# A graph kernel's edge sort: operand layouts, a 32-bit rank copy, a bias by product, and new ticks for the picks

## The chip, the cores and the metric

The kernel runs on one core of a Trainium2 chip. A core has five engines that work through queues of their own: PE (TensorE, matrix products; the loading of its stationary operand is listed as PEld), DVE (VectorE, element-wise work and reductions), ACT (ScalarE, activations and copies), POOL (GpSimd, here indirect transfers) and SP (SyncE, which starts transfers). Products land in PSUM, a memory of eight banks of 512 fp32 values for each of 128 partitions; everything else lies in SBUF. The metric is the device time of one execution in microseconds (us).

## What is computed

Two graph layers over 12,500 nodes of 256 features and 200,000 edges, each with a residual and a layer norm. The change concerns the first layer:

```python
feat = relu(einsum('nd,ohdk->ohnk', feat_in, W) + b[:, :, None, :])
feat_self, feat_nei = feat[0], feat[1]
att_s = leaky(einsum('hnk,hk->hn', feat_self, a_self))
att_n = leaky(einsum('hnk,hk->hn', feat_nei, a_neigh))
edge_w = (att_s[:, row] + att_n[:, col]) * adj_vals
msgs = edge_w[..., None] * feat_nei[:, col, :]
agg = segment_sum(msgs, row, num_segments=N)
...
x = layernorm(x + L0(x, src, dst, edge_weight, ...))
x = layernorm(x + L1(x, edge_index, ...))
```

Here `row` is `src`, `col` is `dst`, and the edges come sorted by `dst`. The sum of the first layer goes over `src`, so the edges have to be brought into another order.

## The kernel before, in words

The kernel has three stages. The first computes the features of the first layer and writes one message per edge into a table in memory (`log`), ordered by the block of 128 source nodes to which the edge belongs. The second reads that table block by block, sums the messages and finishes the first layer. The third is the second layer. All lines of the change lie in the first stage.

The first stage works on groups of 14 tiles of 128 edges; there are 112 groups (`NG`). For each group, `feat_tasks` computes the features of a window of 128 nodes: `transposes` (PE), `keep` (ACT copies them out of PSUM), `project` (PE, L428), `bias` (DVE, L436, adds the bias row), `relu` (ACT, L439), then the attention sums, the centring and, for the first 98 groups, the normalised part of the node block.

`sort_tasks` sorts the group's edges by source block:

- `widen` (ACT, L530) copies each edge's block number 99 times, `hot` (DVE, L534) compares it with 0..98 and so gives the one-hot matrix `A`; `halves` (DVE) adds up its tiles.
- `ranks`, `quarter`, `rows`, `begins` (PE, ACT, DVE, PE) count the edges of each block, round up to rows of four, and give each block's first row and, in the PSUM region `V`, each partition's first place in each block.
- `vhigh` (ACT) and `vlow` (DVE, L571) split `V` into two bf16 parts, which `place_mm` (PE, L588 and L590) spreads over the group's tiles and to which it adds 4096 at each edge's own block. `place_max` then picks that entry: for tiles 0 to 9 by an activation with an accumulator each (ACT, L621), for tiles 10 to 13 by a maximum (DVE, L617, L618). The result is the edge's place among 128 x 16.
- `shift`, `reach`, `steps`, `steps_keep`, `target`, `index` give the row numbers of the table to which the group's rows go.
- `split` (DVE) splits the place into a partition `q` and a column `r`; `hot_r`, `goods`, `hot_q` (DVE, L634, L639, L644) make one-hot matrices of both and multiply the column's by the five values of an edge (`em`); `permute` (PE, L650) is 14 products that put the values in their places.
- `rel_keep`, `extras` (ACT, and DVE L666, L667) read the result. The edge's position in the node window goes through memory (`rel_turn`, `rel_row`, `rel_out`, `rel_in`) and comes back on all partitions; `hot_n` (DVE, L678) makes the one-hot `oT` of it.
- `message(0..5)` (PE, L686) takes the rows of the node features with `oT`, `evict(0..5)` (ACT, L693) copies them into `m`, and `scatter(0..3)` (POOL, L699) writes `m` to the table.

The order on every engine is written by hand. A task has a tick relative to its group; a group begins each 8 ticks (`TG`). Tasks of one tick are issued by group, oldest first, and within a group as listed, sort before features. So about four groups are in work at once, and each engine goes strictly through its own queue. Tasks of the edge data (`meta_tasks`, once per nine groups: load, transpose, block number, the five values, and `twins`, which finds edges of the same block and partition) are issued last in their ticks.

PSUM tiles come by name in turns: `fs` (features, counts and the permuted values of a group), `tp` (transposes), `wp` (places) and `mp` (messages) have two banks each. A new tile waits until all readers of the one that had its bank are done. `ranks` is what takes a group's `fs` bank.

Of the kernel before, what the change touches and what calls it, by code (L numbers as in the profile page):

```python
# [26 lines left out]
P = 128  # L27
# [54 lines left out]
def kernel(  # L82
# [38 lines left out]
    NBX = NB + 1  # L121
    GR = P * NR // RW
# [73 lines left out]
    with ExitStack() as l0:  # L196
# [12 lines left out]
        iotar = dcp.tile([P, NR, GT], BF, name="iotar")  # L209
        later = dcp.tile([P, GT, GT], BF, name="later")  # L210
        identb = dcp.tile([P, P], BF, name="identb")
        identk = dcp.tile([P, P], BF, name="identk")
# [21 lines left out]
        nc.vector.tensor_copy(identb, ident)  # L234
        nc.vector.tensor_single_scalar(identk, ident, BIG, op=OP.mult)
# [5 lines left out]
        nc.vector.tensor_single_scalar(iotar, iotac[:, 0:NR, None].to_broadcast([P, NR, GT]), 0.5 - NR / 2, op=OP.add)  # L241
# [48 lines left out]
        def meta_tasks(c):  # L290
# [4 lines left out]
            def pad():  # L295
                blk[c] = meta.tile([P, TC], BF, name="blk")
                em[c] = meta.tile([P, 5, TC], BF, name="em")
# [4 lines left out]
            def column(i):  # L302
                def f():
# [4 lines left out]
                    st["pt"] = ps.tile([P, 512], FT, name="tp")  # L308
# [14 lines left out]
            def place():  # L323
                nc.vector.scalar_tensor_tensor(em[c][:, 1, :nt], st["s"][:, :nt], -float(P), srcf[:, t0:t0 + nt],
                                               op0=OP.mult, op1=OP.add)
                if full < nt:
                    nc.vector.memset(blk[c][E % P:, full:nt], -1.0)

            def high():
                nc.scalar.copy(em[c][:, 2, :nt], st["adj"][:, :nt])  # L330

            def rest():
                nc.vector.tensor_tensor(st["adj"][:, :nt], st["adj"][:, :nt], em[c][:, 2, :nt], op=OP.subtract)

            def mid():
                nc.scalar.copy(em[c][:, 3, :nt], st["adj"][:, :nt])

            def low():
                nc.vector.tensor_tensor(em[c][:, 4, :nt], st["adj"][:, :nt], em[c][:, 3, :nt], op=OP.subtract)

            def windows():
# [10 lines left out]
                nc.vector.tensor_single_scalar(em[c][:, 0, :nt], rel[:, t0:t0 + nt], 1.0, op=OP.add)  # L352
                if full < nt:
                    nc.vector.memset(em[c][E % P:, 0, full:nt], 0.0)
# [36 lines left out]
        def feat_tasks(g):  # L391
# [12 lines left out]
            def transposes():  # L404
                tp = ps.tile([P, 512], FT, name="tp")
# [18 lines left out]
            def project():  # L424
                fp = bank[g][:, 0:D] if ww else ps.tile([P, 512], FT, name="fs")[:, 0:D]
                for o in range(o0, o1):
                    for c in range(2):
# [3 lines left out]
                            start=(c == 0), stop=(c == 1))  # L431
                st["fp"] = fp

            def bias():
                st["R"] = feat.tile([P, D], FT, name="R")
                nc.vector.tensor_tensor(flat(st["R"]), st["fp"][:, lo:hi], b0b[:, lo:hi], op=OP.add)  # L436

            def relu():
# [1108 lines left out]
```

## Time and profile before

| what | value |
|---|---|
| median of 3 runs | 4602.55 us (4601.2 to 4603.93) |
| the profiled execution | 4600.86 us, its span 4599.1 us |
| PE busy | 3994.0 us, 87% of the span |
| DVE busy | 3407.1 us, 74% |
| ACT busy | 2396.9 us, 52% |
| POOL busy | 2478.5 us, 54% |
| first stage | from the start to about 1,640 us |

The span is the time from the first to the last instruction in the profile. A busy share is a mean over the three stages. In the first stage (400 to 1600 us) PE was busy 1078.8 of 1200 us, DVE 925.7, ACT 759.9 and POOL 374.6, and the mean granted clock of PE was 0.89 of full speed. In lists of instruction groups a row gives line, engine, operation, output and inputs, shapes and count, then busy us and mean ns of one, then the engine's idle time just before them and what ended it. Operations that follow each other on an engine overlap by some hundredths to a tenth of a microsecond. Ends of products are modelled, and an fp32 product is listed as two pieces.

### The profile page before, as it was taken

To read this page: it belongs to the slowest core of one execution; us is meant where nothing else is said; L and a number is where in the kernel's file an instruction comes from. 1 tells how busy PE (TensorE), PEld (TensorE's weight loads), DVE (VectorE), ACT (ScalarE), POOL (GpSimd) and SP (SyncE) were. 2 spreads that over 40 slices of the span, in tenths; PEclk is the share of its full clock that TensorE was granted. 3 is DMA by queue.
4 is the path that set the end of the run, shared out by engine and by line. 5 is a ranking of instruction groups with operands and counts; after the bars stand their busy time and mean duration, and the time that the engine had idled before them with its cause. 6 is when DMAs were issued, how large, how long until landed. Compare 5 with 4: busy or idle time off the path is not lost.

```text
span 4599.1 us, 77987 instructions
## 1 busy us (share of the span) xinstructions
PE 3994.0 (87%) x22817; PEld 3324.8 (72%) x22817; DVE 3407.1 (74%) x10041; ACT 2396.9 (52%) x7507; POOL 2478.5 (54%) x2461
## 2 busy tenths in 40 slices
PE   7988888888889989999999888888788788788876
PEld 5777777777777778888888766666666666666665
DVE  7877777777777688888888666666666666666666
ACT  5666666666666612222222355555555565555555
POOL 1332222322223455554555477777777777777776
PEclk8888888888888999999999999999999999999999
DMA  4555554444443466666666566666666666666664
GB/s 146 192 178 175 179 173 168 146 140 140 148 142 137 140 191 176 176 175 175 176 177 175 150 169 171 171 172 170 170 171 172 169 174 168 169 172 170 172 169 135
DMA packets 453589, 763.31 MB, mean 166 GB/s; under 512 B 75285, under 2 KB 287543, under 8 KB 453159
## 3 DMA queue, kind: packets, MB, share of 16 engines
q1 hardware_dynamic: 322998, 415.17, 31.8%
q0 software_dynamic: 110848, 327.87, 23.0%
q10 hardware_dynamic: 19312, 15.21, 1.0%
q8 instruction: 187, 3.06, 0.3%
q14 instruction: 244, 1.99, 0.1%
HBM read 553.43 MB, written 204.54 MB: 165 GB/s over the span
## 4 chain that ended last, share of the span: by engine, by line
PE 52%; DMA 18%; ACT 11%; DVE 10%; issue 5%; POOL 3%; DVEq 0%; ACTq 0%; POOLq 0%; SPq 0%
PE sum L896 18%; DMA gb<-pd,srcf 17%; PE agg L1294 5%; PE mp L686 5%; PE fs L650 4%; PE wp L588 4%; DVE gb L1275 4%; POOL gb L1216 3%; ACT gb L1277 3%; ACT bx L530 2%; PE qp L1253 2%; PE fs L428 2%; PE qm L984 2%; PE wp L590 2%; PE fs L602 1%
## 5 line engine op out<-in xcount | busy, mean ns | idle before, releaser
L1216 POOL DMA_INDIRECT gb<-pd,srcf x1563 | 1506.6, 964 | 512.6 <-issue 243.8
L699 POOL DMA_INDIRECT log<-m,ix x448 | 490.6, 1095 | 1125.9 <-ACT m L693 783.6
L1294 PE MATMUL agg<-gb,o 128*128 128x256 f32 x3126 | 862.7, 399 | 267.9 <-ACT gb L1277 263.1
L1275 DVE TENSOR_TENSOR gb<-qp,gb 128x512 f32<-128x512 f32 x781 | 538.6, 690 | 650.1 <-DMA gb<-pd,srcf 481.6
L1294 PEld LDWEIGHTS agg<-gb,o 128*128 128x128 f32 x3126 | 554.9, 191 | 497.7 <-ACT gb L1277 439.0
L1277 ACT ACTIVATE gb<-gb 128x512 f32<-128x512 f32 x781 | 491.1, 629 | 791.1 <-DVE gb L1275 788.6
L896 PE MATMUL sum<-lg,o 120*128 120x256 f32 (+1 forms) x3920 | 879.6, 378 | 11.8 <-DMA lg<-log 11.8
L896 PEld LDWEIGHTS sum<-lg,o 120*128 120x128 f32 (+1 forms) x3920 | 732.6, 189 | 116.0 <-POOL lg L883 12.0
L888 DVE TENSOR_SCALAR o<-iotap,lg 120x128 f32<-120x128 f32 (+1 forms) x1960 | 655.8, 400 | 114.2 <-PE sum L896 104.5
L883 POOL TENSOR_TENSOR lg<-lg 120x512 f32<-120x512 f32 x392 | 413.2, 1064 | 455.7 <-DMA lg<-log 230.2
L686 PE MATMUL mp<-F,oT 128*128 128x132 f32 x3584 | 534.4, 288 | 108.1 <-ACT m L693 106.1
L686 PEld LDWEIGHTS mp<-F,oT 128*128 128x128 f32 x3584 | 469.0, 196 | 138.7 <-ACT m L693 128.7
L1253 PE MATMUL qp<-qh,oT 128*128 128x256 f32 x1563 | 543.8, 370 | 2.0 <-DVE oT L1240 2.0
L621 ACT ACTIVATE junk<-wp,nbig 128x99 bf16<-128x99 f32 x1120 | 366.2, 365 | 94.5 <-PE wp L590 94.5
L1253 PE MATMUL qp<-ql,oT 128*128 128x256 f32 x1563 | 406.2, 282 | 0.0
L693 ACT COPY m<-mp 128x396 f32<-128x396 f32 (+1 forms) x672 | 301.2, 454 | 138.0 <-PE mp L686 137.2
L1253 PEld LDWEIGHTS qp<-qh,oT 128*128 128x128 f32 x1563 | 299.3, 192 | 20.1 <-DVE oT L1240 2.4
L1253 PEld LDWEIGHTS qp<-ql,oT 128*128 128x128 f32 x1563 | 299.1, 191 | 17.9
L1240 DVE TENSOR_SCALAR oT<-dr,baseP 128x256 fp32r<-128x256 int32 x782 | 290.0, 371 | 11.1 <-DMA dr<-in_dst_dram 11.1
L1261 ACT ACTIVATE o<-iotac,rel 128x128 f32<-128x128 f32 x782 | 266.0, 387 | 1.5 <-issue 1.5
L650 PE MATMUL fs<-mv,qh 128*128 128x80 bf16 x1568 | 252.4, 328 | 4.7 <-DVE qh L644 4.7
L621 ACT ACTIVATION_READ_ACCUMULATOR junk<-wp,nbig 128x1 f32 x1120 | 253.9, 227 | 0.0
(238 smaller groups left out, 6745.6 us busy)
## 6 DMA issues: line engine op xcount, KB each, us to landing
dr<-in_dst_dram SPq DMA_DIRECT2D x781, 128.0 KB
lg<-log SPq DMA_DIRECT2D x392, 251.2 KB
rr<-reld SPq DMA_DIRECT2D x112, 512.0 KB
log<-zero SPq DMA_DIRECT2D x101, 268.0 KB
lg<-log SPq DMA_DIRECT2D x98, 268.0 KB
gb<-pd,srcf POOLq DMA_INDIRECT x1563, 3.7
xw<-in_x_dram SPq DMA_DIRECT2D x112, 128.0 KB
xw<-x1d SPq DMA_DIRECT2D x112, 128.0 KB
```

Source lines behind the costliest of these rows:

```text
L621: nc.scalar.activation(small("junk", NBX, BF, p=P), w[:, k * NBX:(k + 1) * NBX], AF.Relu, bias=nbig, accum_out=st["sl"][:, a + k:a + k + 1])
L650: nc.tensor.matmul(st["sm"][:, 16:16 + 5 * NR], st["qh"][:, :, t], mv[:, :, t], start=(t == 0), stop=(t == GT - 1))
L686: nc.tensor.matmul(mp[:, r * (HD + H):(r + 1) * (HD + H)], st["oT"][:, r0 + r], F3[g][:, HD:], start=True, stop=True)
L699: ins = nc.gpsimd.indirect_dma_start(out=log[:, :], out_offset=bass.IndirectOffsetOnAxis(ap=st["ix"][:, k:k + 1], axis=0), in_=st["m"][:, ...
L883: e.tensor_tensor(t[:n, 1, :, 0:HD].rearrange("p r (h k) -> p r h k", h=H), t[:n, 0, :, 0:HD].rearrange("p r (h k) -> p r h k", h=H), t[:n ...
L888: nc.vector.tensor_scalar(o[:n, r], iotap[:n], t[:n, 0, r, MW - 2:MW - 1], t[:n, 0, r, MW - 1:MW], op0=OP.is_equal, op1=OP.mult)
L896: nc.tensor.matmul(sums[b], o[:n, r], t[:n, :, r, 0:HD], start=(k == 0 and r == 0), stop=(k == NK - 1 and r == RW - 1))
L1216: nc.gpsimd.indirect_dma_start(out=gb[s][:r, i], out_offset=None, in_=pd[:, :], in_offset=bass.IndirectOffsetOnAxis(ap=srci[:r, t:t + 1], ...
L1253: nc.tensor.matmul(qp[:r, i], oT[:, i * P:i * P + r], q, start=(k == 0), stop=(k == 1))
L1275: nc.vector.tensor_tensor(z, qp, z, op=OP.add)
L1277: nc.scalar.activation(z, z, AF.Relu)
L1294: nc.tensor.matmul(agg[g], o[:r, i], z[:r, i], start=(j == 0 and i == 0), stop=lastmm)
```

## The change

- The edge values `em` are laid out tile by value instead of value by tile, and `hot_r` and `goods` build `rh` and `mv` tile first, so that each product of `permute` reads a contiguous operand. With that the innermost axis of one operand of each is a broadcast.
- `V` gets an even width (`NBE` = 100), is copied once as fp32r by DVE (`keep_v`), and `place_mm` spreads it by one fp32r product in place of two bf16 ones. `begins` issues the product with `less4` first.
- `Z` and the steps are bf16; the steps have a high and a low part (`dh`, `dw`), so `target` issues eight bf16 products in place of four fp32 ones, and `steps_low` is new on DVE.
- The bias row enters `project` as a product of a row of ones with the bias; `bias` is gone, and `relu` reads PSUM.
- `widen` is issued in two halves, at ticks -5 and -4. All 14 picks are activations, spread over ticks 7 to 12. `split` to `hot_q` move from ticks 11 and 12 to 13, `permute` from 14 to 15, `rel_keep` and `extras` from 15 to 16, `rel_turn` to `rel_in` one tick later.
- `tp` has one bank, `mp` three. The metadata tasks get new ticks.

```diff
+    NBE = NBX + NBX % 2
...
-        iotar = dcp.tile([P, NR, GT], BF, name="iotar")
+        iotar = dcp.tile([P, GT, NR], BF, name="iotar")
+        identr = dcp.tile([P, P], FR, name="identr")
...
-                em[c] = meta.tile([P, 5, TC], BF, name="em")
+                em[c] = meta.tile([P, TC, 5], BF, name="em")
...
-                    st["pt"] = ps.tile([P, 512], FT, name="tp")
+                    st["pt"] = ps.tile([P, 512], FT, name="tp", bufs=1)
...
+                nc.tensor.matmul(fp[:, lo:hi], ones[0:1, :], b0b[0:1, lo:hi], start=True, stop=False)
...
-            def bias():
+            def relu():
                 st["R"] = feat.tile([P, D], FT, name="R")
-                nc.vector.tensor_tensor(flat(st["R"]), st["fp"][:, lo:hi], b0b[:, lo:hi], op=OP.add)
-
-            def relu():
-                nc.scalar.activation(flat(st["R"]), flat(st["R"]), AF.Relu)
+                nc.scalar.activation(flat(st["R"]), st["fp"][:, lo:hi], AF.Relu)
...
-            return ((2, transposes), (4, keep), (6, project), (7, bias), (7, k(offsets)), (8, relu),
+            return ((2, transposes), (4, keep), (6, project), (7, relu), (8, k(offsets)),
...
-            def widen():
-                st["bx"] = srt.tile([P, GT, NBX], BF, name="bx")
-                nc.scalar.copy(st["bx"], blk[c][:, tl, None].to_broadcast([P, GT, NBX]))
+            def widen(k):
+                def f():
+                    if k == 0:
+                        st["bx"] = srt.tile([P, GT, NBX], BF, name="bx")
+                    h, t = GT // 2, j * GT + k * GT // 2
+                    nc.scalar.copy(st["bx"][:, k * h:(k + 1) * h],
+                                   blk[c][:, t:t + h, None].to_broadcast([P, h, NBX]))
+                return f
...
+                nc.tensor.matmul(st["V"], r.to_broadcast([NBX, P]), less4[:NBX, :NBE],
+                                 start=True, stop=False)
                 for i, v in enumerate(st["C"]):
-                    nc.tensor.matmul(st["V"], lessb, v, start=(i == 0), stop=False)
-                nc.tensor.matmul(st["V"], r.to_broadcast([NBX, P]), less4[:NBX, :NBX],
-                                 start=False, stop=True)
-
-            def vhigh():
-                nc.scalar.copy(small("vh", NBX, BF, p=P), st["V"])
+                    nc.tensor.matmul(st["V"][:, :NBX], lessb, v, start=False, stop=(i == 3))
+
+            def keep_begins():
                 st["b0"] = begun[:, g:g + 1]
                 nc.scalar.copy(st["b0"], st["sm"][:NBX, 1:2])
 
-            def vlow():
-                nc.vector.tensor_tensor(small("vl", NBX, BF, p=P), st["V"], st["vh"], op=OP.subtract)
+            def keep_v():
+                nc.vector.tensor_copy(small("v", NBE, FR, p=P), st["V"])
...
-                    for k, v in enumerate(("vh", "vl")):
-                        nc.tensor.matmul(o, identb, st[v][:, None, :].to_broadcast([P, n, NBX]),
-                                         start=(k == 0), stop=False)
-                    nc.tensor.matmul(o, identk, st["A"][:, a:a + n],
+                    nc.tensor.matmul(o, identr, st["v"][:, None, :].to_broadcast([P, n, NBE]),
+                                     start=True, stop=False)
+                    nc.tensor.matmul(o[:, :, :NBX], identk, st["A"][:, a:a + n],
                                      start=False, stop=True)
...
-                nc.scalar.copy(small("ds"), st["sm"][:NBX, 2:3])
+                nc.scalar.copy(small("dh", 1, BF), st["sm"][:NBX, 2:3])
+
+            def steps_low():
+                nc.vector.tensor_tensor(small("dw", 1, BF), st["sm"][:NBX, 2:3], st["dh"], op=OP.subtract)
...
-            def place_max(i):
+            def place_pick(*tiles):
                 def f():
...
+                    for t in tiles:
+                        i, k = divmod(t, 5)
+                        if t == 0:
+                            small("sl", GT, p=P)
+                        nc.scalar.activation(small("junk", NBX, BF, p=P), st["w", i][:, k * NBE:k * NBE + NBX], AF.Relu,
+                                             bias=nbig, accum_out=st["sl"][:, t:t + 1])
...
-                st["mv"] = srt.tile([P, NR, 5, GT], BF, name="mv")
-                nc.vector.tensor_tensor(st["mv"], st["rh"][:, :, None, :].to_broadcast([P, NR, 5, GT]),
-                                        em[c][:, None, :, tl].to_broadcast([P, NR, 5, GT]), op=OP.mult)
+                st["mv"] = srt.tile([P, GT, NR, 5], BF, name="mv")
+                nc.vector.tensor_tensor(st["mv"], st["rh"][:, :, :, None].to_broadcast([P, GT, NR, 5]),
+                                        em[c][:, tl, None, :].to_broadcast([P, GT, NR, 5]), op=OP.mult)
...
-                    mp = st["mp", i] = ps.tile([P, 512], FT, name="mp")
+                    mp = st["mp", i] = ps.tile([P, 512], FT, name="mp", bufs=3)
...
-            tasks = [(-4, widen), (-2, hot), (-2, halves), (0, ranks), (1, quarter), (2, rows),
-                     (3, begins), (4, vhigh), (5, vlow), (5, shift), (5, reach), (6, place_mm(0)), (6, place_mm(1)),
-                     (6, steps), (7, place_max(0)), (8, place_max(1)), (8, steps_keep), (9, place_mm(2)),
-                     (10, target), (10, place_max(2)), (11, index), (11, split), (12, hot_r), (12, goods), (12, hot_q),
-                     (14, permute), (15, rel_keep), (15, extras), (16, rel_turn), (17, rel_row), (18, rel_out),
-                     (20, rel_in), (23, hot_n)]
+            tasks = [(-5, widen(0)), (-4, widen(1)), (-2, hot), (-2, halves), (0, ranks), (1, quarter), (2, rows),
+                     (3, begins), (4, keep_begins), (4, keep_v), (5, shift), (5, reach), (6, place_mm(0)),
+                     (6, steps), (7, place_pick(0, 1)), (7, place_mm(1)), (7, steps_keep), (8, place_pick(2, 3, 4)),
+                     (8, steps_low), (9, place_pick(5, 6, 7)), (9, place_mm(2)), (10, target),
+                     (10, place_pick(8, 9)), (11, place_pick(10, 11)), (11, index), (12, place_pick(12, 13)),
+                     (13, split), (13, hot_r), (13, goods), (13, hot_q),
+                     (15, permute), (16, rel_keep), (16, extras), (17, rel_turn), (18, rel_row), (19, rel_out),
+                     (21, rel_in), (23, hot_n)]
```

The tasks after `hot_n` (`message` from tick 25, `evict` from 26, `scatter` from 28) keep their ticks.

## The prediction

> **What bounds the kernel now.** I read the page first (where the time lies), then the busy times by stretch, the waits and the instruction timelines of one group in the first stage. The edits touch only that stage: the first 1,640 of the 4599.1 us, one group of 14 edge tiles after the other, 112 of them.
>
> The busy times by stretch (us; then busy time with instruction counts of PE, PEld, DVE, ACT, POOL; granted clock; DMA share; GB/s):
>
> ```profile
> 400.00:1600.00 1200.00, 1078.81 (x7579) 904.50 (x7579) 925.67 (x2840) 759.92 (x3160) 374.58 (x340) 0.89 0.45 152
> ```
>
> 85 groups ran here (the six-part messages count 85), so a group takes 1200 / 85 = 14.1 us on average. PE is idle only (1200 - 1078.8) / 85 = 1.4 us of it, and its clock is 0.89. From one `begins` to the next (830.66 to 844.38 us) a group without metadata work takes 13.7 us. The waits of 400 to 1600 us (us in total, times, longest) tell what that idle time is:
>
> ```profile
> PE mp L686 <- ACT m L693: 82.2, 75, 1.1
> ...
> DVE R L436 <- PE fs L428: 115.2, 66, 3.0
> ...
> PE fs L548 <- DVE m L667: 13.4, 8, 1.7
> ```
>
> PE waits once per group for a message bank. The timelines of the two engines (start, us, engine) show why:
>
> ```profile
> 831.22 1.54 PE L686 MATMUL mp<-F,oT 128*128 128x132 f32 x12
> 833.90 0.49 PE L686 MATMUL mp<-F,oT 128*128 128x132 f32 x2 [1.14 <-ACT m L693]
> 834.23 2.23 PE L650 MATMUL fs<-mv,qh 128*128 128x80 bf16 x14
> 836.28 0.59 PE L588 MATMUL wp<-vh,identb 128*128 128x495 bf16 x1
> ```
>
> ```profile
> 832.09 1.37 ACT L530 COPY bx<-blk 128x1386 bf16<-128x1386 bf16 x1
> 833.33 0.51 ACT L693 COPY m<-mp 128x396 f32<-128x396 f32 x1
> ```
>
> `widen` holds ACT for 1.24 us, the eviction behind it is late, and PE stands 1.14 us. About two microseconds later the clock halves (stretches of 1 us, columns as above):
>
> ```profile
> 833.00:834.00 1.00, 0.10 (x1) 0.10 (x1) 0.65 (x3) 1.00 (x4) 0.44 (x1) 1.00 0.79 270
> ...
> 835.00:836.00 1.00, 1.00 (x9) 0.94 (x8) 0.93 (x3) 0.00 (x0) 0.08 (x1) 0.86 0.39 154
> 836.00:837.00 1.00, 1.00 (x6) 0.53 (x4) 1.00 (x2) 0.17 (x1) 0.00 (x0) 0.50 0.31 120
> ```
>
> So a group is a PE chain of some 11 us at full clock, a 1.1 us stall, and about 1.5 us lost to half clock. The last wait above shows a second coupling, slack today: `ranks` (L548) cannot reuse a bank before `extras` (L667) of two groups earlier has read it.
>
> **What the Trainium skill says.** (1) "TensorE: Matmul & The Clock Gate", Part 1: the clock has two states, half and full, set by activity in free-running windows of about 3.4 us. The trace agrees: stretches at 0.50 and 1.00, the half ones about 3.3 us long (822.5 to 825.8). (2) "VectorE: DVE Perf Modes", section "What auto-detection actually checks": the double rate needs every 16-bit tensor at step one. The trace agrees: the same 1764 elements take 1.99 us with an innermost broadcast (L362) and 1.07 without (L366). (3) "SBUF — State Buffer", section "Door 1: The DMA port swizzle", note on cachelines: a new 16-byte line at each access costs. `permute` now strides 28 bytes in both operands and takes 2.05 / 14 = 146 ns a pair, where `begins`' contiguous products of 99 columns take about 50 to 65.
>
> ```profile
> L362 DVE TENSOR_TENSOR e<-blk 128x1764 bf16<-128x1764 bf16 x9 | 17.9, 1987 | 0.0
> L366 DVE TENSOR_TENSOR e<-e,later 128x1764 bf16<-128x1764 bf16 x9 | 9.6, 1067 | 0.0
> L639 DVE TENSOR_TENSOR mv<-rh,em 128x1120 bf16<-128x1120 bf16 x86 | 64.0, 745 | 2.9
> L634 DVE TENSOR_TENSOR rh<-iotar,r 128x224 bf16<-128x224 bf16 x85 | 22.9, 269 | 0.0
> L617 DVE TENSOR_REDUCE sl<-wp 128x4 f32<-128x396 f32 x85 | 47.6, 560 | 0.4 <-PE wp L590 0.2
> L436 DVE TENSOR_TENSOR R<-fs,b0b 128x256 f32<-128x256 f32 x71 | 30.0, 422 | 96.2 <-PE fs L428 96.2
> ```
>
> **The change, part by part, for one group.** Lines of two queue neighbours overlap, so I count start to start where the timeline shows it.
>
> PE. Six bf16 products (`vh`, `vl`) become three 32-bit ones: at full clock minus 3 x 0.2 = 0.6 us, if the 32-bit form runs at a column per cycle. The second layer's products of that type start 0.115 us apart for 256 columns, so I take that; at double cost nothing is gained. `permute`: contiguous moving operand, stationary still strided; between 2.05 (stationary is the limit) and 0.9 us; I take 1.2. `target`: eight fp32 pieces in 0.79 us become eight bf16 ones, about 0.5. `project` gains one bias product of 256 columns, about 0.5 (two pieces at twice the 0.125 us of an L428 piece, eight of which take 1.00 us at full clock). Sum -1.2 us, between +0.4 and -1.5: about 9.6 us of PE work, where today 11.
>
> ACT. Four picks more, each 0.32 us after the other (837.80, 838.13): +1.3. `vh` -0.13. `widen` in two halves: +0.1. From about 8.6 to about 9.9 us.
>
> DVE. `bias` -0.35, `place_max(2)` -0.67; `goods` loses the double rate: 1120 elements at L362's 1.13 ns less its fixed part are 1.3 us, +0.57; `hot_r` the same way +0.12; `steps_low` +0.15. Sum -0.2, about 10.7 us. `Z` in 16 bits I cost at nothing (at most +0.25 if it falls to single rate, since L580 now takes 0.49 for 512). The `em` layout touches eight short operations per nine groups: nothing.
>
> Banks. One `tp` fewer, one `mp` more: with that and the split `widen` the 1.14 us stall goes. With one `tp`, transposes wait for `rel_row` on ACT; that sits two instructions behind an eviction and comes about 0.8 us before transposes: nothing. `rel_out` and `rel_in` go one tick later: `rel_in` then leaves about 3.5 us after `extras` and `hot_n` comes at about 11.5, 8 us later, against 7 today (829.24 to 836.20), where L678 waited 0.8 us in all 1200: nothing. POOL's scatters follow the evictions and are idle two thirds of the time.
>
> **What is late next.** No engine is full, so order decides. `permute` moves from tick 14 to 15 and `extras` from 15 to 16. Tick 16 is tick 0 of the group two later, whose `ranks` is there too. Now PE runs `permute`, 4 us of other products, then `ranks`. After the change only one placement product lies between. DVE reaches `extras` only after this queue, from `split`: split 0.6, `hot_r` 0.41, `goods` 1.24, `hot_q` 1.0, shift 0.31, reach 0.40, rstd and norm 0.42, hot 0.90, halves 0.80, `hot_n` 1.19, scale and put 0.55, extras 0.3: 8.1 us. Only then can PE start `ranks`, and everything behind it waits too: messages 0 to 2, the third placement, `target`, transposes, `begins`. And `split` has moved from tick 11 to 13, behind `keep_v` and the last picks. From `extras` to the next `split`: ranks 0.26, message 0.68, `rel_turn` 0.15, placement 0.34, message 0.68 and its latency 0.17: 2.3 us; then on ACT eviction 0.42, two picks 0.64, square 0.2, half a `widen` 0.64 (0.76 from the 512- and 1386-element copies, less overlap), eviction 0.38, two picks with the accumulator's end 0.8: 3.1. Together 5.4 us. Loop: 8.1 + 5.4 = 13.5 us, against 13.7 today. The removed stall comes back as a ring through three engines.
>
> The clock. In this ring PE is idle from the first placement (6.4 us after `extras`) until `shift` gives `steps` its operand (8.9 us): 2.5 us in one piece, and another 0.5 to 1.4 us before `ranks`. Today 1.14 us with the slow `permute` behind it halves the clock in about two cycles of three (the stalls at 904, 925, 949 and 962 us are followed by half clock, those at 919 and 936 are not). I expect one half window in most groups. After the first gap it slows `project` and `permute`, which have about 1 us of slack: about +0.4 through late picks. Over `ranks` to `begins` it costs 1.7 us, in perhaps one group of six: +0.3. So about 14.1 to 14.2 against 13.7 (which has its half windows in it): +0.4 us.
>
> Metadata work adds about 0.37 us per group today (14.1 less 13.7); in the new ring only `twins(0)` (2 us per nine groups) and small casts lie on the DVE leg: 0.3. No change.
>
> Sum: 112 x 0.4 = +45 us on the profiled execution of 4600.86 us (span 4599.1), whose median is 1.7 us higher: about 4646.
>
> **Rivals.**
> 1. The clock stays up (not slower, the other side). The faster, contiguous `permute` lifts activity and few windows trip. For it: some 1.1 us stalls today trip nothing (918.7 us). Against: the gaps are longer. Then a group takes 13.4 us: -0.3 x 112, about 4565. It decides below one half window in three groups.
> 2. The ring does not bind, because PE finds `extras` done earlier than I work out; DVE's 10.7 us plus metadata and some stalls, 12.4 per group on average, would bound: -1.7 x 112, about 4410. For it: DVE is busy only 10.9 of 14.1 us now. Against: the two reuse edges are in the trace.
> 3. Half windows fall on `ranks` to `begins` in half the groups: +0.8 to +1 more, about 4745.
> 4. Stall and ring cancel: 4602.
>
> **How the numbers follow.** Chances: forecast 0.45 (own range 4612 to 4700), rival 3 0.19, rival 4 0.08, rival 1 0.19, rival 2 0.09. This kernel's runs can tell 0.2%, 9 us, from no change. Faster 0.28, same 0.08, slower 0.64. The range leaves out rival 2 and the top of rival 3: 4535 to 4765. The unknown costs (permute, 32-bit product) have slack on PE and move it little.
>
> **What would show it.** Right: L686's wait for ACT gone; instead PE waits for `extras` at `ranks` and for `shift` at `steps`, in nearly every group; PE idle 3 us a group; `goods` near 1.3 us, `permute` near 1.2; clock at or below 0.89; first stage about 45 us longer. Wrong: PE idle below 1.5 us a group, or a clock of 0.97 or more.

## The result, and the profile after

The changed kernel takes 4763.85 us (median of 4 runs, 4758.54 to 4773.0) where the kernel before takes 4602.74 in the same comparison: a ratio of 1.0352, interval 1.0334 to 1.037. The forecast was 4646 us. The direction came as forecast; the step came out at +161 us instead of +45. One of the four executions of a version below (e11) took 17706 us; without it the median of that version is 4628.8 us instead of 4631.7.

All of it lies in the first stage. The last message product starts at 1783.7 us in the trace, at 1614.7 before: +169 us. I call that moment "the end of the first stage" below.

Busy times of the changed kernel from 400 to 1600 us (us; then PE, PEld, DVE, ACT, POOL; granted clock; DMA share; GB/s):

```profile
400.00:1600.00 1200.00, 942.34 (x6859) 788.55 (x6859) 862.25 (x2479) 776.07 (x3500) 346.14 (x308) 0.81 0.42 143
```

77 groups ran here, where 85 ran before: 15.6 us a group. PE stands (1200 - 942.3) / 77 = 3.3 us of it, and its clock fell from 0.89 to 0.81. The waits of the same stretch (us in total, times, longest):

```profile
ACT dh L602 <- PE fs L432: 273.7, 69, 4.6
PE fs L599 <- DVE dl L579: 193.6, 69, 3.3
...
DVE v L576 <- ACT begun L573: 116.4, 77, 2.8
...
PEld L554 <- DVE m L668: 36.9, 43, 2.4
...
PE tp L312 <- DVE v L482: 35.2, 8, 4.5
...
PE fs L554 <- DVE m L668: 20.1, 17, 1.9
```

PE's wait for a message bank, 82.2 us before, is gone. In its place PE waits for `shift` at `steps` (L599, 2.8 us each), in 17 of the 77 groups also for `extras` at `ranks` (L554; 43 count a wait of its weight load), and once in nine groups for the edge data at their transposes (L312, 4.4 us each; in the kernel before 1.1, its line is `PE tp L309 <- DVE mf L307: 9.6, 9, 1.2`). The largest line of PE, DVE and ACT was not in the prediction: ACT waits 4.0 us a group at `steps_keep` (L602). The timeline of ACT shows what stands behind that wait (start, us, engine; in brackets the idle time before it):

```profile
831.32 0.43 ACT L622 ACTIVATE junk<-wp,nbig 128x99 bf16<-128x99 f32 x1
831.56 0.28 ACT L622 ACTIVATION_READ_ACCUMULATOR junk<-wp,nbig 128x1 f32 x1
831.65 0.42 ACT L622 ACTIVATE junk<-wp,nbig 128x99 bf16<-128x99 f32 x1
831.88 0.29 ACT L622 ACTIVATION_READ_ACCUMULATOR junk<-wp,nbig 128x1 f32 x1
836.62 0.16 ACT L602 CAST dh<-fs 99x1 bf16<-99x1 f32 x1 [4.46 <-PE fs L432]
836.68 0.39 ACT L440 ACTIVATE R<-fs 128x256 f32<-128x256 f32 x1
```

Two of the group's 14 picks are done; the other twelve queue behind `steps_keep` and `relu`, which wait until `project` has finished. On PE, `project` stands behind `steps`:

```profile
829.90 0.39 PE L594 MATMUL wp<-A,identk 128*128 128x495 bf16 x1
833.57 0.30 PE L599 MATMUL fs<-dl,step 99*99 99x1 f32 x2 [3.29 <-DVE dl L579]
833.81 0.78 PE L429 MATMUL fs<-b0b,ones 1*128 1x256 f32 x2
834.51 2.07 PE L432 MATMUL fs<-w0s,xT 128*128 128x128 f32 x8
836.38 1.14 PE L651 MATMUL fs<-mv,qh 128*128 128x80 bf16 x14
837.32 0.65 PE L592 MATMUL wp<-v,identr 128*128 128x500 f32 x1
...
840.02 0.35 PE L554 MATMUL fs<-onesb,C 128*99 128x1 bf16 x4 [1.82 <-DVE m L668]
```

After the first gap the clock is at 0.50, and the eight products of `project` take 2.07 us; a second gap stands ahead of `ranks`. This group carries the first part of `twins`, 1.99 us of DVE ahead of `extras`; in the next one (`ranks` at 855.23) the second gap is missing. The instructions that the change touched cost about what was forecast (busy us, mean ns of one, idle before):

```profile
L640 DVE TENSOR_TENSOR mv<-rh,em 128x1120 bf16<-128x1120 bf16 x77 | 102.0, 1325 | 2.6
...
L635 DVE TENSOR_TENSOR rh<-iotar,r 128x224 bf16<-128x224 bf16 x77 | 30.2, 392 | 2.6
```

`goods` 1.33 us (forecast 1.3), `hot_r` 0.39 (0.39). `permute`'s 14 products pass in 0.94 us (836.38 to 837.32), where 1.2 was forecast. One 32-bit placement product of 500 columns keeps the next waiting for 0.34 us where two bf16 ones of 0.21 each (full clock) went before, so the three save some 0.25 us and not 0.6. The bias product takes 0.62 us at full clock (the filled kernel below), 0.5 was forecast. PE's sum stays near the forecast -1.2. The size of the parts is not the error.

**Where the 169 us lie.** The start of `hot_q` (DVE) marks a group in every trace. Nine periods in a row, one round of metadata work (us, worked out from the starts in the traces; "filled", "old ticks" and "hot earlier, filled" are experiments below):

```
before               16.7 13.2 16.3 14.1 15.0 13.2 13.8 13.7 13.7
changed              17.9 15.6 17.9 15.4 14.1 14.1 15.5 16.0 15.3
filled               20.6 14.8 16.0 14.1 14.1 14.1 14.1 14.1 14.1
hot earlier, filled  21.3 14.2 15.2 13.7 13.7 13.7 13.7 13.7 13.7
old ticks            17.3 11.7 15.6 11.3 11.3 11.4 11.3 11.4 11.3
```

From the ninth to the 99th group, 90 periods: before 1292.0 us (14.36 each), changed 1403.9 (15.60), +112. What comes before the ninth group adds 18, the last 13 periods 36 (163.9 to 199.5).

### The profile page after: what moved, and what is told of

It is laid out like the page before. It is cut to its first block, busy times and chain, and to the rows that moved or that the text cites. A ratio compares the mean times of both kernels' runs of the same rounds, so it can differ in the third digit from the quotient of the medians.

```text
span 4771.1 us, 78763 instructions
## 1 busy us (share of the span) xinstructions
PE 3951.4 (83%) x22705; PEld 3290.4 (69%) x22705; DVE 3406.0 (71%) x9818; ACT 2511.6 (53%) x8403; POOL 2496.7 (52%) x2461
## 4 chain that ended last, share of the span: by engine, by line
PE 43%; DMA 18%; DVE 16%; ACT 14%; issue 5%; POOL 3%; DVEq 0%; ACTq 0%; POOLq 0%; SPq 0%
PE sum L899 18%; DMA gb<-pd,srcf 17%; PE agg L1297 5%; ACT junk L622 5%; PE mp L687 4%; DVE gb L1278 3%; PE fs L432 3%; POOL gb L1219 3%; DVE mv L640 3%; ACT gb L1280 3%; DVE qh L645 2%; ACT m L694 2%; PE qp L1256 2%; PE qm L987 2%; PE fs L651 2%
## 5 line engine op out<-in xcount | busy, mean ns | idle before, releaser
L700 POOL DMA_INDIRECT log<-m,ix x448 | 502.5, 1122 | 1281.8 <-ACT m L694 1117.9
L687 PE MATMUL mp<-F,oT 128*128 128x132 f32 x3584 | 558.0, 304 | 4.2 <-DVE lim L769 3.5
L622 ACT ACTIVATE junk<-wp,nbig 128x99 bf16<-128x99 f32 x1568 | 529.5, 357 | 0.9 <-PE wp L594 0.8
L687 PEld LDWEIGHTS mp<-F,oT 128*128 128x128 f32 x3584 | 512.3, 214 | 4.8 <-issue 3.6
L622 ACT ACTIVATION_READ_ACCUMULATOR junk<-wp,nbig 128x1 f32 x1568 | 335.2, 214 | 0.0
L599 PE MATMUL fs<-dl,step 99*99 99x1 f32 x224 | 39.7, 246 | 276.1 <-DVE dl L579 276.1
```

The costliest lines, as they stand in the source:

```text
L622: nc.scalar.activation(small("junk", NBX, BF, p=P), st["w", i][:, k * NBE:k * NBE + NBX], AF.Relu, bias=nbig, accum_out=st["sl"][:, t:t + 1])
L687: nc.tensor.matmul(mp[:, r * (HD + H):(r + 1) * (HD + H)], st["oT"][:, r0 + r], F3[g][:, HD:], start=True, stop=True)
L700: ins = nc.gpsimd.indirect_dma_start(out=log[:, :], out_offset=bass.IndirectOffsetOnAxis(ap=st["ix"][:, k:k + 1], axis=0), in_=st["m"][:, ...
```

## The experiments

The theory after the result: the new order lets `split` come late and closes a ring through several engines, whose length is the period. Its rivals: the parts themselves cost the time (`goods` at single rate, the bias product, 14 picks on ACT); or the lower clock alone does.

Ratios are against the kernel before, run on the same chip. The second set (e5 to e8) and the fourth (e13 to e16) ran on two other chips, where the kernel before takes 4999 and 4969 us. The added time lies behind the first stage (the rest takes 3379 us in e5, 2980 in the changed kernel), so across sets the end of the first stage and the mean period compare, not the totals. The same kernel on two chips (e4, e12) ended its first stage at 1477.4 and 1476.5 us.

| run | ratio, interval | first stage ends | mean period |
|---|---|---|---|
| before | 1 | 1614.7 | 14.36 |
| changed | 1.0352, 1.0334 to 1.037 | 1783.7 | 15.60 |
| e1 three fs banks | 1.0207, 1.019 to 1.0224 | 1715.9 | 15.05 |
| e2 shift ahead | 1.0584, 1.0566 to 1.0602 | 1884.2 | 16.69 |
| e3 old layout | 1.0734, 1.0716 to 1.0752 | 1956.3 | 17.44 |
| e4 before, split widen | 0.9683, 0.9667 to 0.9699 | 1477.4 | 12.99 |
| e5 filled | 1.0205, 1.0188 to 1.0222 | 1724.7 | 15.20 |
| e6 e4 + ranks, targets | 0.9666, 0.9649 to 0.9682 | 1453.6 | 12.72 |
| e7 e4 + layout | 0.9687, 0.967 to 0.9703 | 1448.9 | 12.78 |
| e8 e4 + all three | 0.9663, 0.9647 to 0.968 | 1455.7 | 12.72 |
| e9 changed, old ticks | 0.9606, 0.959 to 0.9622 | 1433.5 | 12.51 |
| e10 permute earlier | 1.0585, 1.0567 to 1.0603 | 1884.1 | 16.68 |
| e11 picks, permute earlier | 1.0056, 1.0036 to 1.0076 | 1635.2 | 14.42 |
| e12 e4 again | 0.9691, 0.9675 to 0.9708 | 1476.5 | 12.96 |
| e13 hot earlier | 1.0205, 1.0188 to 1.0222 | 1721.3 | 15.16 |
| e14 hot earlier, filled | 1.0125, 1.0108 to 1.0142 | 1682.0 | 14.78 |
| e15 metadata apart | 1.0262, 1.0245 to 1.0279 | 1747.8 | 15.34 |
| e16 old ticks, metadata apart | 0.9583, 0.956 to 0.9607 | 1404.8 | 12.20 |
| e17 steps later, hot earlier | 1.0493, 1.0476 to 1.0511 | 1837.2 | 16.21 |
| e18 steps later | 1.0564, 1.0547 to 1.0582 | 1880.0 | 16.63 |

### Is it the order or the parts? (e9, e4, e6, e7, e8, e12)

The changed kernel, with only the sort's ticks put back; every operation stays as changed, `widen` stays halved:

```diff
-  (6, place_mm(0)), (6, steps), (7, place_pick(0, 1)), (7, place_mm(1)), (7, steps_keep), (8, place_pick(2, 3, 4)),
-  (8, steps_low), (9, place_pick(5, 6, 7)), ... (12, place_pick(12, 13)), (13, split), (13, hot_r), (13, goods), (13, hot_q),
-  (15, permute), (16, rel_keep), (16, extras), (17, rel_turn), (18, rel_row), (19, rel_out), (21, rel_in),
+  (6, place_mm(0)), (6, place_mm(1)), (6, steps), (7, place_pick(0, 1, 2, 3, 4)), (8, place_pick(5, 6, 7, 8, 9)),
+  (8, steps_keep), (8, steps_low), (9, place_mm(2)), (10, target), (10, place_pick(10, 11, 12, 13)), (11, index),
+  (11, split), (12, hot_r), (12, goods), (12, hot_q), (14, permute), (15, rel_keep), (15, extras), (16, rel_turn), ...
```

> The changed kernel with all its operations, and only the ticks of the sort put back as they were before (first two placements at tick 6, picks in threes bursts at 7, 8 and 10, split 11, hot_r to hot_q 12, permute 14, extras 15); widen stays in two halves. Theory (the new order makes the ring, the operations themselves cost little): the first stage ends near that of the versions of the old order with the parts added, 1450 to 1500 us, so 4440 to 4530 us in all. Rival (the bias product on PE, or all 14 picks on ACT, cost the time): 4620 us or more.

Measured: 4423.74 us, ratio 0.9606, below the expected span and 182 us faster than the kernel before. So the new order alone turns a gain of 4% into a loss of 3.5%. The waits of this kernel (same stretch) show ACT's stall gone; `relu` still waits for `project`, but for half a microsecond, because five picks and more stand ahead of it:

```profile
ACT R L440 <- PE fs L432: 27.8, 60, 0.5
```

Do the parts gain, then? The kernel before, with `widen` in two halves, one `tp` bank and three `mp` banks, and the third metadata transpose a tick earlier:

```diff
-            tasks = [(-4, widen), (-2, hot), ...
+            tasks = [(-5, widen(0)), (-4, widen(1)), (-2, hot), ...
-  ps.tile([P, 512], FT, name="tp")            mp: ps.tile([P, 512], FT, name="mp")
+  ps.tile([P, 512], FT, name="tp", bufs=1)    mp: ps.tile([P, 512], FT, name="mp", bufs=3)
```

> The kernel before with only this of the change: widen in two halves at ticks -5 and -4, one bank for tp, three for mp (and the third metadata transpose one tick earlier, which one bank needs). If the wait of 1.1 us for a message bank and the half clock behind it are what a group of the kernel before loses, both go: 1.5 to 2.5 us a group, total 4320 to 4430. If another wait takes its place at once (rival), the total stays within 50 us of 4603.

Measured 4458.17 us, ratio 0.9683 (again in e12, 4464.37 us). These small edits together remove the 1.14 us stall and are worth 137 us of the first stage. To it were added the 32-bit rank copy with the 16-bit targets (e6), the contiguous layout (e7), and all three (e8):

```diff
+  e6: keep_v as fp32r, one product with identr in place of vh and vl; Z, dh and dw in bf16, steps_low at 9
+  e7: em [P, TC, 5], rh [P, GT, NR], mv [P, GT, NR, 5], permute reads mv[:, t]
```

> The kernel of e4 (old order, split widen, three message banks) with two of the change's parts: the 32-bit rank copy and the 16-bit targets. They take about 0.9 us from PE and add 0.15 to DVE. If the parts are sound and only the new order is bad: 20 to 90 us below e4, total 4370 to 4440. Rival 'DVE already sets e4's pace' (permute waited 0.3 us a group for hot_q): within 20 us of 4458 or up to 20 slower.

> The kernel of e4 with the change's layout alone: permute reads contiguous operands (-1.0 us on PE), goods and hot_r at single rate (+0.7 us on DVE, ahead of permute). Theory that DVE stands ahead of permute: +20 to +80 us over e4 (4480 to 4540). Rival 'the layout is a gain wherever PE is the fuller engine': 50 to 100 us below e4.

> The kernel of e4 with the rank copy, the 16-bit targets and the layout together, in the order of the kernel before. If the changes add up, e6 plus e7's difference; with 1.9 us less on PE and 0.85 more on DVE the pace is DVE's: 4440 to 4540. If it is below e6, the layout pays once PE is relieved; above 4603 would mean that the parts and not the order made the change slow.

> The version of before with widen in two halves, one tp bank and three mp banks, on the chip of the other three, for their comparison: 4458 us, as measured before.

The first stage ended 24, 28 and 22 us earlier than in e4. Each part alone gives about 0.2 us a group, and together they give no more; in e8 DVE is busy 1083 of 1200 us, so it probably sets the pace. The layout was to cost 20 to 80 us by my theory of DVE, or to gain 50 to 100 by its rival; it gained 28, and neither held. The two parts that e8 lacks, the bias by product and all picks on ACT, take work from DVE; e9 has them and ends its first stage 22 us earlier than e8.

### Which ring sets the pace? (e5, e1, e14, e13, e10, e11)

To see the ring without half clock, useless products (ten of 512 columns ahead of `steps`, five after the second placement) were put into PE's gaps:

```diff
-  (6, steps), (7, place_pick(0, 1)), (7, place_mm(1)), (7, steps_keep),
+  (6, fill(10)), (6, steps), (7, place_pick(0, 1)), (7, place_mm(1)), (7, fill(5)), (7, steps_keep),
```

> The changed kernel, with products of no use (ten of 512 columns before steps, five behind the second placement product) that fill PE's two idle stretches of a group and write to a bank nobody reads. They remove no wait and shorten nothing. Theory 'the ring is near 13.5 us at full clock and the rest is half clock behind the gaps': the first stage's clock rises from 0.81 to 0.95 or more and the total falls to 4540 to 4640. Rival 'the ring itself is 15 us or more, whatever the clock': the total stays at 4764 or rises, since the fillers can only delay.

The clock is 0.98, as expected, and the first stage ends at 1724.7, 59 us earlier. Expected were 124 to 224 us, so the theory held for the clock and not for the time. The 59 us are a lower bound for what the half clock costs, because the fillers also delay. In the groups with the metadata transposes PE comes late to the fillers, and they stand ahead of `steps` although `shift` has been done since 642.5 us:

```profile
643.35 0.30 PE L312 MATMUL tp<-ident,mf 126*128 126x126 f32 x1 [4.37 <-DVE v L482]
...
644.35 0.63 PE L602 MATMUL tp<-iotab,identb 128*128 128x512 bf16 x1
645.21 2.97 PE L602 MATMUL tp<-iotab,identb 128*128 128x512 bf16 x8 [0.22 <-issue]
648.01 0.26 PE L607 MATMUL fs<-dl,step 99*99 99x1 f32 x2
```

That is 3.7 us (644.35 to 648.01) once in nine groups, 0.4 us a group. Outside metadata work, where `steps` still waits for `shift` and not for the fillers, a constant period of 14.07 us is left. The timeline of DVE in this kernel gives the two legs:

```profile
596.77 0.17 DVE L637 SCALAR_TENSOR_TENSOR sl<-sl,twin 128x14 f32<-128x14 f32 x1
...
604.72 0.20 DVE L676 TENSOR_REDUCE m<-fs 128x16 f32<-128x48 f32 x1
...
610.67 0.26 DVE L576 CAST v<-fs 128x100 fp32r<-128x100 f32 x1 [1.47 <-ACT begun L573]
610.85 0.16 DVE L637 SCALAR_TENSOR_TENSOR sl<-sl,twin 128x14 f32<-128x14 f32 x1
```

From `split` to the end of `extras` 604.92 - 596.77 = 8.15 us (forecast 8.1), from there to the next `split` 5.93 (forecast 5.4). In nearly every group (79 of 80) the weight load of `ranks` now waits for `extras`.

A third `fs` bank should free `ranks` from waiting for `extras`; one `mp` bank had to be given up for it:

```diff
-  bank[g] = ps.tile([P, 512], FT, name="fs")            mp: name="mp", bufs=3
+  bank[g] = ps.tile([P, 512], FT, name="fs", bufs=3)    mp: name="mp", bufs=2
```

> The changed kernel with three banks for fs and two for mp, so that ranks takes a bank that was read a whole group earlier. Ring theory (DVE from split to extras, then ranks, messages and picks back to split): the ring is cut at extras -> ranks, a group of the first stage falls from 15.6 us by 2 us or more, total below 4600. Rival 'half clock alone' (the gap before steps is what costs): that gap of 2.5 us stays, total within 60 us of 4764. Rival 'DVE is the bound' (goods and hot_r at single rate): within 40 us of 4764. If two mp banks bring the old wait back, PE waits for ACT at the messages by 1 us a group and the gain is 100 us smaller.

4700.92 us, not under 4600. The wait for a message bank came back (97.6 us at PE's products, and at its weight loads as in the line below), so this run does not decide:

```profile
PEld mp L687 <- ACT m L694: 114.4, 92, 1.9
```

A cleaner cut is to shorten only DVE's leg: `hot` and `halves` (1.7 us of it) go to tick -5, where DVE waits for `keep_v`; `widen` goes a whole group earlier, so ACT's order stays.

```diff
-            tasks = [(-5, widen(0)), (-4, widen(1)), (-2, hot), (-2, halves), (0, ranks), ...
+            tasks = [(-13, widen(0)), (-12, widen(1)), (-5, hot), (-5, halves), (0, ranks), ...
```

> The same with the useless products of the filled kernel, which take the half clock away: its period between metadata groups was 14.07 us. Theory: 12.4 to 13.0 us. Rival: 13.7 to 14.1 us.

> The changed kernel with hot and halves at tick -5 instead of -2 and widen at -13 and -12 (one group earlier, so ACT's order stays as it is). They leave DVE's leg from split to extras (8.1 us, of which hot and halves are 1.7) and stand where DVE waits for keep_v anyway. Theory (the ring split, DVE, extras, ranks, placement, picks, split sets the pace): the period falls by 1 to 1.7 us, 4570 to 4660 us in all. Rival (another ring binds, split, hot_q, shift, steps, permute, second placement, picks, split, in which hot and halves do not stand; or the clock): within 60 us of the changed kernel, 4700 us or more.

With the fillers the period fell from 14.07 to 13.71 us only, which was the rival's number: `extras` no longer sets it, and another ring stands 0.36 us behind. Its timeline, DVE and then ACT:

```profile
595.53 0.16 DVE L637 SCALAR_TENSOR_TENSOR sl<-sl,twin 128x14 f32<-128x14 f32 x1
...
597.82 1.08 DVE L653 TENSOR_TENSOR qh<-iotaq,q 128x1792 bf16<-128x1792 bf16 x1
598.82 0.21 DVE L579 SCALAR_TENSOR_TENSOR dl<-pos,capc,begun 99x1 f32<-99x1 f32 x1
...
609.24 0.16 DVE L637 SCALAR_TENSOR_TENSOR sl<-sl,twin 128x14 f32<-128x14 f32 x1
```

```profile
601.17 0.16 ACT L610 CAST dh<-fs 99x1 bf16<-99x1 f32 x1 [2.90 <-PE fs L432]
601.22 0.39 ACT L440 ACTIVATE R<-fs 128x256 f32<-128x256 f32 x1
601.99 0.17 ACT L664 CAST rs<-fs 128x16 bf16<-128x16 f32 x1 [0.38 <-PE fs L659]
602.06 0.35 ACT L630 ACTIVATE junk<-wp,nbig 128x99 bf16<-128x99 f32 x1
```

`split` to `shift` 3.29 us (`hot_r`, `goods` and `hot_q` stand between them on DVE), `shift` through `steps` and `project` on PE to `steps_keep` 2.35, then on ACT `relu`, `rel_keep` and twelve picks, among evictions and half a `widen`, to the next `split` 8.07: together 13.71. Here `split` stands in tick 13, which is tick 5 of the next group, `shift`'s own. Without fillers (e13) the first stage got 62 us shorter, where 104 to 194 were expected, with shortest periods of 14.0 us.

Permute, `extras` and what follows one tick earlier, so that `extras` leaves the tick of `ranks` (e10); and, in e11, the picks packed to end at tick 11 and `split` to `hot_q` at 12 as well:

```diff
-  (13, split), ... (13, hot_q), (15, permute), (16, rel_keep), (16, extras), (17, rel_turn), (18, rel_row), (19, rel_out), (21, rel_in)
+  e10: (14, permute), (15, rel_keep), (15, extras), (16, rel_turn), (17, rel_row), (18, rel_out), (20, rel_in)
+  e11: the same, and (12, split), ... (12, hot_q), picks three a tick at 7 to 10, two at 11, (8, place_mm(2))
```

> The changed kernel with permute, rel_keep and extras and what follows them (to rel_in) one tick earlier, 14 and 15, and all else as changed, so that extras no longer stands in the tick of the ranks that reuse its bank. Theory (the ring closes at ranks waiting for extras): PE's waits at L554 for extras go, and the group gains 0.5 to 1.5 us, 4590 to 4710 us in all. Rival (permute then waits longer for hot_q on PE, and the half clock grows, as it did with shift moved ahead): 4760 us or more.

> As the one before, and also the picks end one tick sooner (three to a tick from 7 to 10, two at 11, the third placement at 8) and split to hot_q stand at tick 12. Theory: the time between split and permute is two ticks as in the changed kernel, so hot_q is not late and extras is out of the tick of ranks: 4450 to 4600 us. Rival (ACT cannot do three picks a tick beside the evictions, or the clock decides): within 60 us of the changed kernel, 4700 us or more.

In e10 the waits at `ranks` for `extras` are gone, as the theory said, and the kernel still took 4875.71 us: PE now waits for `hot_q` in 64 of 71 groups, with the next group's first placement behind it, and the clock fell to 0.74.

```profile
PEld L651 <- DVE qh L645: 219.5, 64, 3.9
PE fs L651 <- DVE qh L645: 207.2, 64, 3.7
```

The rival's number held. In e11, with the picks and `split` one tick sooner, this wait fell to 117.5 us in 73 groups, the shortest period to 12.3 us and the time to 4631.7 us: not the 4600 of the theory, but 244 us below e10. The picks, the third placement and `split` moved together here, so the run shows what an earlier `split` with its picks is worth, not which of the moves did it.

### Cutting the waits at `steps` (e2, e17, e18)

`shift` and `reach` at tick 4, ahead of `split` (e2); then, leaving `shift`, the second placement at tick 6 and `steps_keep` at 8, with `hot` earlier (e17) and without (e18):

```diff
-  e2: (5, shift), (5, reach)
+  e2: (4, shift), (4, reach)
-  e17, e18: (6, steps), (7, place_pick(0, 1)), (7, place_mm(1)), (7, steps_keep), (8, place_pick(2, 3, 4)), (8, steps_low)
+  e17, e18: (6, place_mm(1)), (6, steps), (7, place_pick(0, 1)), (8, place_pick(2, 3, 4)), (8, steps_keep), (9, steps_low)
```

> The changed kernel with shift and reach at tick 4, ahead of split to hot_q on DVE, so that steps and project on PE need not wait for hot_q. Ring theory: shift and reach only change place inside the ring's DVE leg, the total stays within 60 us of 4764, although the 2.5 us wait at steps goes and turns up at permute. Rival 'the wait at steps is the loss': 2.5 us x 112 = 280 us less, total about 4500.

> The changed kernel with hot and halves earlier (as in the two runs before), and with the second placement at tick 6, ahead of steps, and steps_keep at tick 8 behind three picks (steps_low at 9), so that on PE the second placement no longer stands behind steps and permute and on ACT the picks no longer stand behind the wait for steps. Two-ring theory (one ring through extras and ranks at 14.07 us, one through shift, steps and permute at 13.7 us, both cut here): shortest periods of 12 to 13 us instead of 14, ratio 0.99 to 1.01 to before. Rival (the half clock or permute's wait for hot_q holds the period up): ratio 1.02 or more, as with hot and halves alone.

> The same without the earlier hot and halves: only the ring through shift, steps and permute is cut. Two-ring theory: the ring through extras and ranks still binds at 14.07 us, so the shortest periods stay there and the ratio stays at 1.025 to 1.04. Rival (the waits at steps alone were the loss): ratio 1.00 or less.

All three are slower than the changed kernel, and no theory's number held; only the rival of e17 (1.02 or more) did. In e2 the wait went to `ranks` (PE, L554 for `extras`: 163.0 us in 64 groups), and the clock fell to 0.77. In e17 the wait at `steps_keep` became one at `relu`, which stands in tick 7 and needs `project` just as well:

```profile
ACT R L440 <- PE fs L432: 275.0, 65, 5.4
```

So this edit did not cut the second ring, though I had expected it to, and the clock fell to 0.75. On PE the second placement now stands ahead of the wait at `steps` and no longer behind `permute`; that this lowers the clock is likely, but not shown. A version with `relu` behind the picks too wasn't tried.

### The layout alone in the new order (e3)

The changed kernel with the old order of `em`, `rh` and `mv`:

```diff
-  mv [P, GT, NR, 5], read as mv[:, t]
+  mv [P, NR, 5, GT], read as mv[:, :, t]
```

> The changed kernel with the old layout of em, rh and mv: goods and hot_r at double rate again, the products of permute with a moving operand of stride 28 bytes. Ring theory: DVE's leg is 0.7 us shorter and permute 0.9 us longer, but permute has slack: about 0.7 us a group less, total 4660 to 4720. Rival 'DVE's lost rate is the whole slowdown': total back at 4600 or below. If permute decides (it stands before extras), no change or slower.

4942.01 us, against an expected 4660 to 4720. `goods` was back at its double rate, as planned, but the slow `permute` (2.0 us in the group shown, at half clock) stands ahead of `rel_keep`, and the half clock then lasts for about ten microseconds (stretches of 1 us, columns as above):

```profile
816.00:817.00 1.00, 1.00 (x4) 0.48 (x3) 0.97 (x3) 0.00 (x0) 0.00 (x0) 0.50 0.47 189
...
820.00:821.00 1.00, 1.00 (x7) 0.68 (x5) 0.09 (x2) 0.30 (x2) 0.00 (x0) 0.50 0.59 210
...
824.00:825.00 1.00, 1.00 (x5) 0.98 (x5) 0.00 (x0) 0.71 (x5) 0.00 (x0) 0.50 0.02 3
```

In this order the contiguous layout saves the changed kernel 173 us of the first stage (1956.3 to 1783.7).

### The metadata work (e15, e16)

In the filled kernel nine groups take 9 x 15.20 us where 9 x 14.07 would do: metadata costs 1.13 us a group there, of which 0.4 is the fillers' delay shown above. Most of it is in the groups with the transposes (20.6 us). A column's cast (DVE), transpose (PE) and copy (ACT) stood at the end of one tick; they were put into ticks of their own:

```diff
-  (28, 27, 26, 24, 25, 22, 20, ...): pad, column(0), column(1), block, column(2), place, high, ...
+  (29, 29, 29, 29, 28, 27, 26, 25, 23, 22, 20, 19, 17, ...): pad, cast(0..2), turn(0), column(0), turn(1), column(1), block, place, turn(2), column(2), high, ...
```

> The changed kernel with each metadata column's cast (DVE), transpose (PE) and copy (ACT) in ticks of their own instead of all three at the end of one tick. Theory (of the 1.1 us a group that metadata costs in the filled kernel, the 6.6 + 0.7 us of the groups with the transposes are waits of PE for the cast behind DVE's queue): 0.4 to 0.8 us a group less, 4675 to 4720 us. Rival (it is the work itself): within 25 us of the changed kernel.

> The version with the old ticks (4423.74 us, where two of nine groups took 17.3 and 15.5 us instead of 11.3) with the metadata columns taken apart in the same way. Theory: 4345 to 4385 us. Rival: 4400 us or more.

Both gained about half of the expectation: 0.26 and 0.31 us a group, 36 and 29 us of the first stage. In e15 the waits of PE at the transposes fell from 35.2 to 16.2 us (of 1200). With the old ticks the group of 17.3 us became ones of 12.4 to 12.6; the 15.5 us of the group with `twins` stayed. So part of the metadata term was waits between engines, and part is work. e16 is the best version of all: ratio 0.9583, first stage 1404.8 us.

## Why the prediction was wrong in its sum, and right in its order

**Right.** L686's wait for ACT went; PE waits at `steps` for `shift` in 69 of 77 groups; PE idles 3.3 us a group (forecast 3); `goods`, `hot_r`, `steps_low` and `Z` (0.475 us, no change) cost what was said; the clock is below 0.89. That the order and not the parts makes the kernel slow was the prediction's main claim, and e9 shows it. The ring through `extras` and `ranks` is real (e5, e14), but at `ranks` the changed kernel itself waits in 17 groups only, not in nearly every one.

**Wrong: the sum 112 x 0.4.** Measured over 90 groups it is 1.24 us a group:

| term, us a group | forecast | measured |
|---|---|---|
| period at full clock, against before | 13.5 - 13.7 = -0.2 | 14.07 - 13.78 = +0.29 |
| half clock in the new order | about +0.65 | 15.60 - 15.20 = +0.40, up to about +0.8 |
| metadata, against before | 0.3 - 0.37 = -0.07 | 1.13 - 0.58 = +0.55, down to about +0.15 |
| sum | +0.4 | +1.24 |

(13.78 is the median period before; 14.36 - 13.78 = 0.58 is then its metadata term. The split of the changed kernel's 15.60 takes the filled kernel as the one without half clock. The second values of the two middle rows count the fillers' 0.4 us as no metadata; how the two share their 0.95 is not settled closer than that.)

1. "Loop: 8.1 + 5.4 = 13.5 us" was 0.57 us short, all in the way back from `extras` to `split` (5.93 instead of 5.4). In the filled kernel, from the end of `extras` (604.92) to the second eviction (607.53) there are 2.6 us instead of 2.3: a message took 0.85 instead of 0.68 until the next product, and the third placement 0.47 instead of 0.34. From there to the end of the last pick (610.58) the forecast 3.1 us held. Then `keep_begins` and `keep_v` stand ahead of `split` (610.85), another 0.27; the prediction named `keep_v` and gave it no time. So the ring alone is already longer than the period before, where the forecast's slowdown came from the clock alone.
2. A second ring was missing. `steps_keep` went from tick 8 to 7, ahead of twelve picks, and ACT waits 4.0 us a group there. At full clock this ring is 13.71 us, so even a shorter `extras` ring would not have gone below that (e14).
3. "Metadata work adds about 0.37 us [...] No change" was too small on both sides. The 14.1 us behind it are a mean that counts the lighter last groups; over the groups with features it is 14.36, and metadata costs 0.58. After the change it costs more, and part of that is PE's wait at the transposes (35.2 us in 1200, 9.6 before), some of which ticks alone take out (e15, e16). The new order is not needed for it: in e4 and e9 mean less median period is 1.05 and 1.17 us. Whether the stall of the kernel before had hidden this work, or its second `tp` bank helped, no run tells apart.
4. All 112 groups were taken as alike. The last groups have no block features: before, their periods drop to 163.9 / 13 = 12.6 us; in the changed kernel they stay at 199.5 / 13 = 15.3. Filling the gaps takes 21 of these 36 us back (199.5 to 178.5, with periods down to 12.9), so most of it is half clock. What comes before the ninth group adds 18.

The half clock itself was forecast about right. The third placement, which lies between `ranks` and `begins`, ran at half clock (0.70 us instead of 0.45) in 19 of 77 groups; the forecast had one in six, rival 3 (4745 us) every second one. So that rival's time came near in part by luck.

Rivals 1 and 2 fell by the trace: the clock is lower, and the ring does bind. What stays open is whether one edit to the changed order (for instance `relu` and `steps_keep` both behind the picks) would break both rings; e10, e17 and e18 each left or made another.

## What to carry to other kernels

When tasks change their ticks, walk every queue once from the first to the last of the moved instructions and write down what stands ahead of what: one short instruction that waits (here a cast of 99 values) holds all picks behind it. Close every ring that the new order makes, not only the one that looks longest, and take the length of periodic work from the groups that carry it, not from a mean over all groups. When several edits arrive with a new order, put the edits into the old order first: here that alone was worth 182 us against before.

## What the runs showed of the hardware

- The half clock follows a gap of 3.29 us in the changed kernel and already one of 1.14 us (with slow products behind it) in the kernel before; without that stall (e4) the clock was 0.94 instead of 0.89. The Trainium skill, "TensorE: Matmul & The Clock Gate", section "Why this matters for your kernels", warns of idle gaps over about 3 us; by these traces shorter ones can be enough. In e3 the half clock then stayed from about 815.4 to 825.7 us though PE was busy in nearly all of it.
- Useless products hold the clock (0.98 instead of 0.81) and bring the end of the first stage forward by 59 us, though once in nine groups they delay `steps` by 3.7 us.
- A 32-bit product of 500 columns with its own weights keeps PE 0.34 us at full clock, against 0.21 us for a bf16 one of 495; in the second layer's long rows 256 columns took 0.115.
- A contiguous moving operand brings a weight load and product of 80 columns from 0.146 to 0.067 us (`permute`, 14 pairs; before, mostly at full clock), with the stationary operand strided in both.
